# A graph network's first layer: one more block gathered, one fewer multiplied, and blocks built in another order

## The chip, the cores and the metric

The kernel runs on one core of one Trainium2 chip. The metric is the device time of one execution in microseconds (us); smaller is better. The engines are called by the profile's names: PE (matrix multiplies; PEld its weight loads), DVE (VectorE), ACT (ScalarE), POOL (GpSimd) and SP (which issues most DMAs).

## The reference

Four layers of message passing over 6250 nodes of 256 channels with 100000 edges sorted by destination, behind a layer norm and in front of a residual add:

```python
def agg(h):
    return jax.ops.segment_sum(h[src], dst, num_segments=N)      # N = 6250, 100000 edges
h = jnp.maximum(_layernorm(x), 0.0)
for l in range(3):
    t = h + agg(h)
    t = relu(t @ W1s[l] + b1s[l]); t = relu(t @ W2s[l] + b2s[l])
    h = t @ W3s[l] + b3s[l]
t = h + agg(h)
t = relu(t @ cW1 + cb1); t = relu(t @ cW2 + cb2)                 # cW2: 256 x 64
return x + t @ cW3 + cb3
```

## The kernel before

Nodes are cut into 49 blocks of 128. A layer's sum over edges is made in one of two ways for each block of destinations:

- A **gathered** block is made by a *visit*. POOL sends 17 indirect DMAs (L1407, `rows<-table,idx`), each of which fetches 128 source rows from the layer's table in DRAM; then PE adds them with 23 multiplications by a matrix of zeros and ones (L1446, `sums<-rows,hot`). `gath` has 24 buffers for such rows.
- A **multiplied** block uses its block row of the adjacency matrix: 49 matrices of 128 x 128 edge counts, each multiplied with one block of `XY` (the features as two halves, 512 columns). In the first layer these are 49 *products* of 128x512 at L1622 (`agg<-XY,a`); in later layers four blocks go together (L1700).

The adjacency counts are not given; they are **built** during the first layer for 30 blocks (18 to 47). For one block `build` runs 16 batches of two *steps*. For a batch DVE writes two tiles of zeros and ones, `lo` and `hi` (L1053, two buffers each). A step is two multiplications of 128x196 on PE (L1094, `bp<-hi,lo`, three buffers in PSUM) and one copy of the result into the block's counts `at` (three buffers): ACT copies the first step of a batch (L1102), DVE the second (L1104). DVE's order in a batch is `lo` and `hi` of the next batch, then the copy. A finished block is written to DRAM (SP, `mat<-at`) for the later layers; where the first layer multiplies it, ACT also turns it into 13 tiles `a` (L1582): twelve carry four products, the last one product. A tile with its products is called a *unit*.

Instructions stand in the order that the program text gives (no scheduler). A planner in Python decides that order: it counts units (`now`) and a clock worked out from fixed costs (`clock`), places visits and the two-stage dense layers (L1256, L1313) between units, and before each unit emits build steps:

```python
total = GSUB * len(made)
g0, u1 = GSUB + EARLY, steps - len(node_parts[-1]) - AHEAD - 1
goals = [min(g0 + (total - g0) * u // u1, total) for u in range(1, steps + 1)]
...
goal = min(goals[at - PRE], built[0] + 3)
while built[0] < goal and free_of(built[0] // GSUB - 3):
    next(beside)
    built[0] += 1
```

So the number of steps built follows a straight line over the units, at most three steps go ahead of one unit, and a block may be begun only when the block three places earlier in the list `made` has been turned into its `a` tiles (a block that the first layer doesn't multiply counts as free at once). `made` is the order in which blocks are built. `teams` are the multiplied blocks of the first layer, put through the dense layers together; `teams[0]` also decides how many blocks of the group 16 to 19 are gathered.

For visits, `begin` sets a pace at which rows are asked for and visits fall due; the plan ends `TAIL[l]` clock units ahead of the layer's worked-out end:

```python
self.end = begun[self.l] + work_of(self.l) - TAIL[self.l]
self.pace = (self.end - clock[0] - MARGIN) / self.upto[-1]
```

Of the kernel before, what the change touches and what calls it, by code (L numbers as in the profile page):

```python
# [396 lines left out]
def sorted_edges(  # L397
# [41 lines left out]
    NLAYER = W1s.shape[0]  # L439
# [29 lines left out]
    panels = [(20, 4), (24, 4), (28, 4), (32, 4), (36, 4), (40, 4), (44, 4)]  # L469
# [3 lines left out]
    S0 = 2 * min(place_of)  # L473


    teams = [(18, 2), (20, 4), (24, 4), (28, 4), (32, 4), (36, 4), (40, 2), (42, 2)]
    made = [b + i for b, n in teams for i in range(n)]
    for i in range(panels[-1][1]):
        made.insert(6 * i + 5, panels[-1][0] + i)
    assert sorted(made) == sorted(place_of) and sum(gone[-3]) == panels[0][0] and gone[-2] == panels[-1] and all(n == gone[0][1] for _, n in gone[:-1]) and sorted(  # L480
        b + i for b, n in gone[:-2] + gone[-1:] + panels for i in range(n)) == list(range(NT))
    NQ = len(gone)
# [498 lines left out]
    with tc.manual_schedule():  # L981
# [376 lines left out]
        class Gathered:  # L1358
# [30 lines left out]
            def begin(self):  # L1389
                self.one_hots(0)  # L1390
                self.end = begun[self.l] + work_of(self.l) - TAIL[self.l]
                self.pace = (self.end - clock[0] - MARGIN) / self.upto[-1]
# [139 lines left out]
        spare = clT.rearrange("p a q s -> p (a q s)").bitcast(F32)  # L1532
        sums = ps_g.tile([P, W], F32, name="sums")
        MARGIN = 6.0
        TAIL = [10.0] + [-5.0] * (NLAYER - 1) + [10.0]
        LATE = [-8] + [10] * (NLAYER - 1) + [-8]
        COLS, FULL32, TURN, VISIT, BUILD, BURST = 0.457e-3, 1.68e-3, 0.4, 3.0, 0.2, 0.3
        clock = [0.0]
# [10 lines left out]
        def work_of(l):  # L1549

            t = (len(nodes) if l == 0 else sum(stock[p][1] for p in order[l])) * NT * W * COLS
            t += len(layers[l].blocks) * (len(ROUNDS) * VISIT + TURN)
            for k, n in ((l, NT - tails[l]), (l - 1, tails[l - 1])):
                mid = NOUT if k == NLAYER else C
                t += (k >= 0) * n * (P * KC + C) * FULL32 * (2 if mid == C else 0.5)
            t += 2 * (len(gone) + (len(teams) if l == 0 else len(panels)) - 1) * BURST
            if l == 0:
                t += BUILD * GSUB * len(made) + TURN * len(nodes)
            return t
# [205 lines left out]
def kernel(  # L1765
# [26 lines left out]
    good = keep.tile([1, 1], I32, name="good")  # L1792
    rest = (x, src, dst, W1s, b1s, W2s, b2s, W3s, b3s, cW1, cb1, cW2, cb2, cW3, cb3, out)
    sorted_edges(tc, good, *rest)
    done = nc.values_load(good[0:1, 0:1], min_val=0, max_val=1)
    with tc.If(done == 0):
# [27 lines left out]
```

## Time and profile before

| | us |
|---|---|
| median of 3 runs | 2127.4 (2123.55 to 2129.25) |
| profiled execution, its own time | 2128.08 |
| profiled execution, its span | 2126.3 |
| PE busy in the span | 2034.3 |
| DVE busy | 925.0 |
| ACT busy | 872.8 |
| POOL busy | 1445.9 |

The span has three parts: normalisation and look-up of edges to about 116 us, the first layer to 690.8 us (the first L1700 product), and three later layers. Instructions of one kind are grouped by their source line; "idle before" is the time for which the engine stood still just ahead of them, and the name behind it is what ended that. A timeline row gives the start, the length, the line and the tiles, and in brackets the idle time ahead.

### The profile page before, as it was taken

Reading aid. Unit: us, or ns where it says so; the run is one execution under the profiler, and the core shown is the slowest. Engines: PE = TensorE matmul, PEld = TensorE weight load, DVE = VectorE, ACT = ScalarE, POOL = GpSimd, SP = SyncE. Lnnn points to the kernel's source line nnn. Section 1 sums busy time; section 2 is a strip of 40 time slices with the busy share of each in tenths; the row PEclk is TensorE's granted clock in tenths of the full one; section 3 lists DMA queues with packets and bytes.
Section 4 is the critical chain, followed back from the end, with each engine's and each line's share of the span. In section 5 each row is a group of like instructions: output and inputs, shape, how many; then the busy total and the mean of one; then the engine's idle time right before and its main releaser. Section 6 shows DMA issues by size and latency. Waiting matters only on the chain.

```text
span 2126.3 us, 33236 instructions
## 1 busy us (share of the span) xinstructions
PE 2034.3 (96%) x12076; PEld 1495.9 (70%) x12076; DVE 925.0 (44%) x2103; ACT 872.8 (41%) x1793; POOL 1445.9 (68%) x1467
## 2 busy tenths in 40 slices
PE   6889999999999999999999999999999999989998
PEld 4657676667676777777777777777776767766665
DVE  6987767677662422232234322322233323223333
ACT  5766656456555433323233423232233322222222
POOL 3747777677774477777777477777776477777772
PEclk9989999999999999999999999999999999999999
DMA  5534455545455654555566554555555555555563
GB/s 174 159 117 148 145 156 150 157 139 162 140 161 168 205 163 145 160 177 161 154 184 202 171 165 149 176 166 158 169 171 176 173 170 185 161 184 185 154 189 109
DMA packets 184900, 347.54 MB, mean 163 GB/s; under 512 B 32446, under 2 KB 118496, under 8 KB 184726
## 3 DMA queue, kind: packets, MB, share of 16 engines
q0 software_dynamic: 68960, 185.36, 29.9%
q1 hardware_dynamic: 113838, 158.12, 22.8%
q8 instruction: 96, 1.57, 0.3%
q10 hardware_dynamic: 1928, 1.85, 0.3%
q14 instruction: 78, 0.64, 0.1%
HBM read 287.93 MB, written 57.26 MB: 162 GB/s over the span
## 4 chain that ended last, share of the span: by engine, by line
PE 86%; DMA 4%; DVE 3%; issue 1%; ACT 1%; POOL 1%; DVEq 0%; SPq 0%; POOLq 0%; ACTq 0%
PE agg L1700 43%; PE agg L1622 15%; PE sums L1446 11%; PE ps L1256 6%; PE ps L1313 6%; PE bp L1094 4%; DMA rows<-table,idx 4%; PE ps L1506 1%; DVE hi L1053 1%; POOL rows L1407 1%; DVE at L1104 1%; PE ps L1268 1%; PE ps L1248 0%; DVE lo L1053 0%; ACT at L1102 0%
## 5 line engine op out<-in xcount | busy, mean ns | idle before, releaser
L1407 POOL DMA_INDIRECT rows<-table,idx x1394 | 1388.8, 996 | 595.7 <-issue 225.7
L1700 PE MATMUL agg<-a,XY 128*128 128x512 f32 x4116 | 978.6, 395 | 1.9 <-DVE clT L1634 1.9
L1700 PEld LDWEIGHTS agg<-a,XY 128*128 128x128 f32 x4116 | 764.9, 188 | 192.7 <-issue 35.0
L1598 ACT CAST a<-at 128x512 fp32r<-128x512 uint8 (+1 forms) x542 | 328.7, 617 | 653.7 <-PE agg L1700 613.1
L1598 DVE CAST a<-at 128x512 fp32r<-128x512 uint8 x543 | 246.8, 456 | 515.7 <-PE agg L1700 479.1
L1622 PE MATMUL agg<-XY,a 128*128 128x512 f32 x1470 | 405.4, 410 | 1.7 <-ACT a L1582 1.0
L1622 PEld LDWEIGHTS agg<-XY,a 128*128 128x128 f32 x1470 | 260.0, 190 | 51.4 <-issue 6.6
L1446 PE MATMUL sums<-rows,hot 128*32 128x256 f32 x3772 | 248.3, 391 | 33.5 <-DMA rows<-table,idx 33.3
L1446 PEld LDWEIGHTS sums<-rows,hot 128*32 128x32 f32 x3772 | 124.0, 111 | 151.0 <-DMA rows<-table,idx 46.1
L1582 ACT CAST a<-at 128x512 fp32r<-128x512 uint8 (+2 forms) x362 | 197.2, 576 | 6.6 <-PE agg L1622 6.6
L1102 ACT CAST at<-bp 128x392 uint8<-128x392 f32 x252 | 121.5, 490 | 186.9 <-PE bp L1094 181.3
L1104 DVE CAST at<-bp 128x392 uint8<-128x392 f32 x228 | 128.6, 564 | 137.4 <-PE bp L1094 135.0
L1475 DVE TENSOR_TENSOR u<-u,sums 128x256 f32<-128x256 f32 x82 | 34.4, 419 | 301.3 <-PE agg L1700 273.6
L1094 PE MATMUL bp<-hi,lo 128*128 128x196 bf16 x960 | 128.3, 256 | 14.9 <-DVE hi L1053 13.3
L1313 PE MATMUL ps<-w,h 128*128 128x256 f32 x588 | 133.8, 379 | 1.4 <-ACT h L1259 0.9
L1053 DVE TENSOR_TENSOR hi<-cols,pairs 128x784 bf16<-128x784 bf16 x240 | 134.9, 562 | 0.0
L1256 PE MATMUL ps<-h,w 128*128 128x512 f32 (+3 forms) x332 | 133.8, 545 | 0.3 <-ACT h L1713 0.3
L1094 PEld LDWEIGHTS <-lo 128*128 128x128 bf16 x960 | 72.3, 100 | 83.5 <-DVE hi L1053 34.9
L1313 PEld LDWEIGHTS ps<-w,h 128*128 128x128 f32 x588 | 111.3, 190 | 18.5 <-ACT h L1259 1.4
L1321 DVE TENSOR_TENSOR zz<-ps,w 128x512 f32<-128x512 f32 (+1 forms) x75 | 50.2, 679 | 116.5 <-PE ps L1313 116.5
L1053 DVE TENSOR_TENSOR lo<-lanes,pairs 128x512 bf16<-128x512 bf16 x240 | 100.6, 419 | 0.7 <-issue 0.3
L1510 ACT ACTIVATE h<-ps,bias 128x256 f32<-128x256 f32 (+1 forms) x116 | 47.6, 464 | 128.5 <-PE ps L1506 128.5
(170 smaller groups left out, 962.6 us busy)
## 6 DMA issues: line engine op xcount, KB each, us to landing
at<-mat SPq DMA_DIRECT2D x151, 448.0 KB
mat<-at SPq DMA_DIRECT2D x30, 784.0 KB
rows<-table,idx POOLq DMA_INDIRECT x1394
table<-zz SPq DMA_DIRECT2D x72, 256.0 KB
back<-table SPq DMA_DIRECT2D x99, 128.0 KB
xs<-in_x_dram SPq DMA_DIRECT2D x8, 768.0 KB
table<-zs SPq DMA_DIRECT2D x24, 256.0 KB
out_dram<-zz SPq DMA_DIRECT2D x24, 256.0 KB
```

The lines of the kernel that those rows point to most:

```text
L1053: nc.vector.tensor_tensor(o.rearrange("p q (n t) -> p q n t", t=2), values.rearrange("p (n t) -> p n t", t=2)[:, None, :, :].to_broadcast( ...
L1094: mm = nc.tensor.matmul(bp[:, m * HW:(m + 1) * HW], lo[:, q + m, :], hi[:, q + m, :], start=True, stop=True)
L1102: nc.scalar.copy(o, v)
L1104: nc.vector.tensor_copy(o, v)
L1256: mm = nc.tensor.matmul(ps[:mp, :w], weights[l][0][:, c, i * P:i * P + mp], h1[:, c, :w], start=(c == 0), stop=(c == KC - 1))
L1313: mm = nc.tensor.matmul(o, h2[0][:, c, nodes], w3[:, c, :], start=(c == 0), stop=(c == KC - 1))
L1407: got = nc.gpsimd.indirect_dma_start(out=t, out_offset=None, in_=tables[self.l][:, :], in_offset=bass.IndirectOffsetOnAxis(ap=idx[:, o:o + ...
L1446: nc.tensor.matmul(self.sums[m * Q:(m + 1) * Q, :C], self.hot[:, c - min(rounds), m, :], self.rows[g, c + 4 * m], start=(c == ROUNDS[0][0] ...
L1582: nc.scalar.copy(a[:, i * m * P:(i + 1) * m * P].rearrange("p (j d) -> p j d", j=m), counts[b][:, j:j + m, :])
L1598: cast(o, at[:, :, d:d + m * P])
L1622: mm = nc.tensor.matmul(agg, a[:, d:d + P], XY[:, j, :], start=(j == 0), stop=(j == NT - 1))
L1700: mm = nc.tensor.matmul(agg[c][:, :w], XY[:, j, o:o + P], a[:, :w], start=(at == 0 and half == 0), stop=(at == NT - 1 and half == 1))
```

## The change

Block 18 moves from the multiplied blocks to the gathered ones, so that 24 are gathered and 25 multiplied. Its counts are still built, since the last layer multiplies it, but last of all instead of first. The four blocks 44 to 47, built and not multiplied in the first layer, each stand one place later among the others. The plan of visits of the first layer ends 16 clock units ahead of the layer's worked-out end, not 10.

```diff
-    teams = [(18, 2), (20, 4), (24, 4), (28, 4), (32, 4), (36, 4), (40, 2), (42, 2)]
+    teams = [(19, 1), (20, 4), (24, 4), (28, 4), (32, 4), (36, 4), (40, 2), (42, 2)]
     made = [b + i for b, n in teams for i in range(n)]
     for i in range(panels[-1][1]):
-        made.insert(6 * i + 5, panels[-1][0] + i)
+        made.insert(6 * i + 6, panels[-1][0] + i)
+    made.append(18)
@@
-        TAIL = [10.0] + [-5.0] * (NLAYER - 1) + [10.0]
+        TAIL = [16.0] + [-5.0] * (NLAYER - 1) + [10.0]
```

From the `append` on, each line of the changed kernel has a number one higher (L1622 is L1623, L1094 is L1095).

Three places show how the rows move. The names are tiles with their numbers; `x4` is four instructions in a row.

PE in the middle of the first layer, before: one unit's four products, then two build steps (four multiplications and their weight loads), then the next four products.

```order
L1622 MATMUL agg_6094<-XY_71,a_6023 128x512 x4
L1094 LDWEIGHTS lo_6096
L1094 MATMUL bp_6124<-hi_6102,lo_6096 128x196
L1094 LDWEIGHTS lo_6096
L1094 MATMUL bp_6124<-hi_6102,lo_6096 128x196
L1094 LDWEIGHTS lo_6096
L1094 MATMUL bp_6130<-hi_6102,lo_6096 128x196
L1094 LDWEIGHTS lo_6096
L1094 MATMUL bp_6130<-hi_6102,lo_6096 128x196
L1622 MATMUL agg_6094<-XY_71,a_6031 128x512 x4
```

PE in the middle of the first layer of the changed kernel: these twelve rows are all that stands between four products ahead of them and one product behind them.

```order
L1095 LDWEIGHTS lo_5569
L1095 MATMUL bp_5591<-hi_5575,lo_5569 128x196
L1095 LDWEIGHTS lo_5569
L1095 MATMUL bp_5591<-hi_5575,lo_5569 128x196
L1095 LDWEIGHTS lo_5569
L1095 MATMUL bp_5597<-hi_5575,lo_5569 128x196
L1095 LDWEIGHTS lo_5569
L1095 MATMUL bp_5597<-hi_5575,lo_5569 128x196
L1095 LDWEIGHTS lo_5589
L1095 MATMUL bp_5605<-hi_5595,lo_5589 128x196
L1095 LDWEIGHTS lo_5589
L1095 MATMUL bp_5605<-hi_5595,lo_5589 128x196
```

Three build steps stand ahead of one unit where two stood. Behind the first 24 steps, 216 units have two steps ahead of them before and 8 have three; in the changed kernel 102 have three, 70 have two and 10 have one.

PE a few rows further on in the changed kernel: one build step, and then units with none.

```order
L1095 LDWEIGHTS lo_5649
L1095 MATMUL bp_5692<-hi_5655,lo_5649 128x196
L1095 LDWEIGHTS lo_5649
L1095 MATMUL bp_5692<-hi_5655,lo_5649 128x196
L1623 MATMUL agg_5613<-XY_71,a_5609 128x512 x4
L1623 MATMUL agg_5613<-XY_71,a_5637 128x512 x4
L1623 MATMUL agg_5613<-XY_71,a_5667 128x512 x4
L1623 MATMUL agg_5613<-XY_71,a_5698 128x512 x4
L1623 MATMUL agg_5613<-XY_71,a_5704 128x512 x4
L1623 MATMUL agg_5613<-XY_71,a_5714 128x512 x4
L1623 MATMUL agg_5613<-XY_71,a_5722 128x512 x4
```

After a stretch of groups of three steps, seven units follow each other without a step; before, the units without a step stood one by one between the others.

SP's DMAs at the end of the first layer, before (`mat_95` holds the counts of blocks 40 to 43, `mat_90` those of 20 to 23, `table_84` is the second layer's table, and `back` brings rows of it back to be split):

```order
L516 DMA table_84<-zz 128x2x256 x2
L1109 DMA mat_95<-at 896x1x896 x2
L516 DMA table_84<-zz 128x2x256
L1109 DMA mat_95<-at 896x1x896
L1127 DMA at<-mat_90 128x3584
L516 DMA back<-table_84 128x256 x5
L516 DMA table_84<-zz 128x2x256 x2
L516 DMA back<-table_84 128x256 x7
```

SP's DMAs at the same place of the changed kernel:

```order
L517 DMA table_84<-zz 128x2x256 x2
L1110 DMA mat_95<-at 896x1x896 x3
L517 DMA table_84<-zz 128x2x256
L517 DMA table_84<-zz 128x256
L1128 DMA at<-mat_90 128x3584
L517 DMA back<-table_84 128x256 x3
L1110 DMA mat_97<-at 128x6272
L517 DMA table_84<-zz 128x2x256 x2
L517 DMA back<-table_84 128x256 x9
```

The write of block 18's counts (`mat_97`) was the first of all such writes and is now the last, with two table writes and nine `back` reads behind it. POOL asks for 408 tiles of rows in the first layer where it asked for 391, and PE has 49 products of L1622 fewer and 23 multiplications of L1446 more. From the first L1700 product on, PE's rows are the same in both kernels.

## The prediction, made blind

> **What bounds the kernel now.** I read the page first, then the busy time by stage, the waits and groups of the first layer, and the timelines of PE and DVE where a few microseconds decide.
>
> ```profile
> span 2126.3 us, 33236 instructions
> PE 2034.3 (96%) x12076; PEld 1495.9 (70%) x12076; DVE 925.0 (44%) x2103; ACT 872.8 (41%) x1793; POOL 1445.9 (68%) x1467
> ```
>
> PE bounds the whole. By windows (start and end, length, then busy time of PE, PEld, DVE, ACT and POOL with the number of instructions, granted clock, DMA share, GB/s):
>
> ```profile
> 116.00:122.00 6.00, 0.77 (x9) 0.69 (x10) 4.79 (x14) 0.80 (x3) 1.15 (x1) 0.75 0.13 37
> 122.00:134.00 12.00, 9.86 (x50) 5.24 (x48) 10.84 (x27) 10.42 (x27) 7.60 (x7) 0.50 0.60 200
> 200.00:640.00 440.00, 432.24 (x2940) 304.42 (x2940) 308.45 (x697) 258.71 (x584) 323.22 (x323) 1.00 0.51 152
> 549.20:554.20 5.00, 4.33 (x31) 3.02 (x30) 4.41 (x12) 3.68 (x9) 3.78 (x5) 1.00 0.75 228
> ```
>
> In the body of the first layer PE is busy 432.2 of 440 us and DVE 308.5: DVE has 30% to spare as a mean. The second layer's order on PE is unchanged, so the whole difference is made here. The only PE waits in the first layer that matter are two (total, times, longest):
>
> ```profile
> PE bp L1094 <- DVE hi L1053: 7.2, 12, 1.4
> PE sums L1446 <- DMA rows<-table,idx: 2.4, 1, 2.4
> ```
>
> The first, 7.2 us between 134 and 640 us, is PE waiting for DVE's ones-and-zeros tiles. The last row of the windows is one such place, where before already has two groups of three build steps one after the other. PE there:
>
> ```profile
> 549.25 0.69 PE L1094 MATMUL bp<-hi,lo 128*128 128x196 bf16 x6
> 549.71 1.18 PE L1622 MATMUL agg<-XY,a 128*128 128x512 f32 x4
> 550.73 0.34 PE L1094 MATMUL bp<-hi,lo 128*128 128x196 bf16 x2
> 551.23 0.51 PE L1094 MATMUL bp<-hi,lo 128*128 128x196 bf16 x4 [0.16 <-DVE hi L1053]
> 551.53 1.17 PE L1622 MATMUL agg<-XY,a 128*128 128x512 f32 x4
> 552.54 0.51 PE L1094 MATMUL bp<-hi,lo 128*128 128x196 bf16 x4
> 552.84 0.48 PE L1622 MATMUL agg<-XY,a 128*128 128x512 f32 x1
> 553.83 0.51 PE L1094 MATMUL bp<-hi,lo 128*128 128x196 bf16 x4 [0.51 <-DVE hi L1053]
> ```
>
> And DVE, which is idle at first and then never:
>
> ```profile
> 549.80 0.57 DVE L1104 CAST at<-bp 128x392 uint8<-128x392 f32 x1 [0.59 <-PE bp L1094]
> 550.28 0.41 DVE L1053 TENSOR_TENSOR lo<-lanes,pairs 128x512 bf16<-128x512 bf16 x1
> 550.61 0.56 DVE L1053 TENSOR_TENSOR hi<-cols,pairs 128x784 bf16<-128x784 bf16 x1
> 551.11 0.57 DVE L1104 CAST at<-bp 128x392 uint8<-128x392 f32 x1
> 551.93 0.56 DVE L1053 TENSOR_TENSOR hi<-cols,pairs 128x784 bf16<-128x784 bf16 x1
> 552.40 0.56 DVE L1104 CAST at<-bp 128x392 uint8<-128x392 f32 x1
> 553.21 0.56 DVE L1053 TENSOR_TENSOR hi<-cols,pairs 128x784 bf16<-128x784 bf16 x1
> 553.69 0.56 DVE L1104 CAST at<-bp 128x392 uint8<-128x392 f32 x1
> ```
>
> Copy to copy is 1.29 us (551.11, 552.40, 553.69): that is DVE's price of a batch (two build steps). PE starts a batch's first row 0.05 to 0.06 us after DVE ends its `hi` (551.17, 552.49 and 553.77, against 551.23, 552.54 and 553.83). On PE six building multiplications, three steps, take 0.46 us (549.25 to 549.71), so a step is 0.15; four products take 1.02 (549.71 to 550.73), one takes about 0.32. A unit with two steps therefore costs PE 0.30 + 1.02 = 1.32 us and DVE 1.29: balanced, and the units without steps between them let DVE catch up. A unit with three steps costs PE 1.47 and DVE 1.94.
>
> **The change part by part.**
>
> *Products and visit.*
>
> ```profile
> 651.49 2.80 PE L1446 MATMUL sums<-rows,hot 128*32 128x256 f32 x46
> 654.22 5.74 PE L1622 MATMUL agg<-XY,a 128*128 128x512 f32 x24
> 659.80 0.60 PE L1506 MATMUL ps<-ident,un 128*128 128x128 f32 x4
> ```
>
> 24 products take 659.80 - 654.22 = 5.58 us, 0.2325 each; 49 fewer give -11.4 us. One more visit costs 654.22 - 651.49 = +2.7 us. Block 18's transposes and dense layers move from a pair to a group of three and leave block 19 alone; the columns are the same: 0. ACT loses 13 casts and isn't waited for: 0.
>
> *The end of the plan.* The last visit of the layer waited 2.4 us for its rows. The changed plan paces rows so that they end 6 units sooner; I take the wait as gone, -2.4, between -2.4 and 0.
>
> *The build steps.* This is the term that decides. The steps are the same 480, but in the changed order they stand in 102 groups of three (8 before), because the straight line of the plan is now steeper (as many steps over 13 units fewer) and 18 and 44 to 47 stand further back: the builder gets to its limit of three `at` buffers, stops, and makes up for it at three steps a unit when a block's casts are through. A run of such groups is bound by DVE. How much PE waits follows from the place above. When a run starts, the tiles of the first two batches are ready. DVE begins the first copy 0.55 us after PE's first build row (549.25 to 549.80), so batch i (from 0) can start at 0.55 + (i - 1) x 1.29 + 0.06, the last for the step from DVE to PE; for i = 2, 3 and 4 that is 1.90, 3.19 and 4.48 us, and the trace has 1.98, 3.29 and 4.58 (551.23, 552.54, 553.83). PE alone would be there after 0.15 per step and the products between. With "n" the groups that follow each other without a visit or a dense layer between:
>
> - n = 2 (last batch is i = 2): ready 1.90, PE alone 1.62; wait 0.3. There are 5: 1.5 us.
> - n = 3 (i = 4): ready 4.48, PE alone 3.24, or 2.54 where one unit has a single product; wait 1.2 (four) or 1.9 (one): 6.7 us.
> - n = 4 (i = 5): ready 5.77, PE alone 3.86 with a single-product unit; wait 1.9 (three), 1.2 (one): 6.9 us.
> - n = 5 (i = 7; the usual one, most of a block in one go): ready 8.35; PE alone 14 x 0.15 + 3 x 1.02 + 0.32 = 5.5; wait 2.9. There are 9: 26.1 us.
> - n = 9, once: ready 0.61 + 12 x 1.29 = 16.1, PE alone 11.4; 4.7 us. Seven groups stand alone: 0.
>
> That is 45.9 us of new waiting, in runs that last 9.5 + 22.4 + 23.1 + 75.2 + 16.1 = 146 us together. PE doesn't get it back: in the stretches without steps it runs at its own rate, and there DVE idles, since its two buffers of `lo` and `hi` let it be one batch ahead and no more.
>
> *DVE's other work in those runs.* In the body of the layer (134 to 640 us):
>
> ```profile
> L1430 DVE TENSOR_TENSOR hot<-colf,rel 128x768 f32<-128x768 f32 x21 | 20.0, 952 | 0.0
> L1321 DVE TENSOR_TENSOR zz<-ps,w 128x512 f32<-128x512 f32 x18 | 11.6, 682 | 0.0
> L1634 DVE TENSOR_TENSOR un<-un,agg 128x256 f32<-128x256 f32 x23 | 9.6, 415 | 1.3 <-ACT un L1630 1.3
> L1466 DVE TENSOR_TENSOR u<-XY 128x256 f32<-128x256 f32 x21 | 8.8, 419 | 3.7 <-PE ps L1506 3.7
> L1475 DVE TENSOR_TENSOR u<-u,sums 128x256 f32<-128x256 f32 x21 | 8.7, 413 | 0.0
> L1108 DVE TENSOR_TENSOR at<-at,ident 128x128 uint8<-128x128 uint8 x28 | 8.2, 293 | 4.2 <-ACT at L1102 1.2 <-ACT pairs L1048 0.5
> ```
>
> 66.9 us in 506, or 0.13 us in each. What falls into a run adds to the wait in full: 146 x 0.13 = 19; a little less, since these rows overlap the next one's start: I take +16, between 0 and 30 (they may cluster between runs or in them).
>
> *Waits of before.* The 7.2 us belong to units of two and three steps; of those with two, 70 are left of 216. I take -4.8, between -7.2 and 0.
>
> *POOL and SP.* POOL has 17 tiles more to ask for:
>
> ```profile
> L1407 POOL DMA_INDIRECT rows<-table,idx x362 | 363.7, 1005 | 145.6 <-issue 57.8 <-PE bp L1094 43.7 <-PE agg L1622 34.0
> 663.25 0.96 POOL L1407 DMA_INDIRECT rows<-table,idx  x1 [0.30 <-issue]
> 664.52 0.95 POOL L1407 DMA_INDIRECT rows<-table,idx  x1 [0.31 <-issue]
> ```
>
> At its fastest it asks every 1.27 us (663.25 to 664.52); 408 x 1.27 = 518 us. The layer gave it 506 us for 362, or 1.40 each, and will be longer: 0.
>
> ```profile
> mat<-at SPq DMA_DIRECT2D x30, 784.0 KB
> ```
>
> On SP the write of block 18's counts (784 KB, at the 228 GB/s of the fourth window about 3.5 us of transfer) now stands ahead of the last table writes; its block is complete over 20 us sooner by PE's order (at least 52 products of 0.23 and a visit stand between), so I give it 0, and up to 3.
>
> The sum: -11.4 + 2.7 - 2.4 + 45.9 + 16 - 4.8 = +46.0 us. The profiled execution took 2128.1 (span 2126.3), 0.7 above the median of the runs, so 2128.1 + 46.0 = 2174.
>
> **The rivals.**
>
> *DVE stays hidden.* If the steps' tiles were ready anyway, only PE's own work would count: 2128.1 - 11.4 + 2.7 - 2.4 = 2117. For it: DVE is idle 30% of the body as a mean, and the two waits at the place above are small. Against it: that place shows DVE without a pause from 549.80 and PE held by it at the third and the fifth batch; the mean says nothing of a run. It would decide if runs were of one or two groups, but 19 of the 31 are longer. Chance 0.04.
>
> *Half of it.* If runs are cut up by waits elsewhere (a late `a` tile, a full PSUM buffer), so that DVE catches up inside them: half of 45.9 + 16, 2128.1 - 11.4 + 2.7 - 2.4 - 4.8 + 31 = 2143. Chance 0.08.
>
> *PE's clock falls.* In a run of five PE works 5.5 of 8.35 us, 66%. The windows show 1.00 granted at 87% (4.33 of 5.00 us) and 0.50 right after a stretch at 13% (0.77 of 6.00): 66% lies between, nearer to the first, and with gaps of under 1 us each. At half clock the five units of a run would take PE 11 us where DVE takes 8.35: 2.7 more a run, and for 102 groups, twenty times five, +54: 2228. Chance 0.04. The Trainium skill has this rule in "TensorE: Matmul & The Clock Gate", under "A second HAM failure mode: psum-queue depth-cycling": small idle gaps between groups of multiplications can make the clock swing between half and full. By that rule the time would be 2228; the fourth window, with such gaps at full clock, speaks against it here.
>
> **How the numbers follow.** The forecast has 0.83: 2174. Its own bounds: small DVE work 0 and all of the old waits gone, -11.4 + 2.7 - 2.4 - 7.2 + 45.9 = +27.6, or 2156; small work 30, none of the old waits or of the last visit's gone and SP's 3, -11.4 + 2.7 + 45.9 + 30 + 3 = +70, or 2198. The other cases lie outside (2117 and 2143 below, 2228 above) and have 0.16 together, 0.01 is left for what I don't see, so the range of 2156 to 2198 has about 8 in 10. A change of 0.3% (6 us) is about what a measurement of this kernel can tell from none. Faster by more than that: 0.04, the hidden DVE. Within: 0.01. Slower: 0.95.
>
> **What the profile after would show.** PE's wait for DVE's `hi` at L1095 should grow from 7.2 to some 60 to 70 us, in clusters of 3 to 4 us, once for nearly each multiplied block, with DVE's copies 1.29 us apart in them. PE's busy time should fall by about 9 us, the first L1701 product should come near 737 us instead of 690.8 (below), and what lies behind it should last as long as before. I am wrong if PE's wait for `hi` stays under 30 us, if the granted clock in the body of the first layer falls below 0.95, or if visits wait for rows.
>
> ```profile
> 690.81 1.21 PE L1700 MATMUL agg<-a,XY 128*128 128x512 f32 x4 [1.85 <-DVE clT L1634]
> ```

## The result, and the profile after

| | before | after |
|---|---|---|
| median of 4 runs, us | 2125.48 (2123.44 to 2129.25) | 2182.88 (2174.47 to 2184.61) |
| profiled execution, own time, us | 2128.08 | 2174.47 |
| span, us | 2126.3 | 2172.7 |
| first layer, 116 us to the first product of the second, us | 574.8 | 626.9 |
| from there to the end of the span, us | 1435.5 | 1429.8 |

The ratio is 1.0257 with a 95% interval of 1.0232 to 1.0282: slower, by some 49 to 60 us between medians. The profiled execution of the changed kernel was the shortest of its four; profile against profile the loss is 46.4 us. Only the profiled one can be looked into, so the accounting below is of 46.4; where the others spend 7 to 10 us more is not known. The mean granted clock doesn't tell: it is 0.986 in the profiled execution and 0.985 in the others, which is about 2 us by estimate.

The page's busy times of the changed kernel:

```profile
PE 2041.0 (94%) x12073; PEld 1495.5 (69%) x12073; DVE 923.8 (43%) x2105; ACT 877.1 (40%) x1782; POOL 1464.3 (67%) x1484
```

The waits of PE over its whole span (total, times, longest):

```profile
PE bp L1095 <- DVE hi L1054: 60.5, 87, 5.2
PE sums L1447 <- DMA rows<-table,idx: 24.8, 14, 4.5
```

The same two waits over the whole span of before:

```profile
PE sums L1446 <- DMA rows<-table,idx: 33.3, 15, 6.2
PE bp L1094 <- DVE hi L1053: 13.3, 15, 5.2
```

The wait for DVE's `hi` has grown by 47.2 us (60.5 against 13.3), all of it in the first layer; DVE as a whole has no more to do than before. The first product of the second layer in the changed kernel:

```profile
742.86 1.16 PE L1701 MATMUL agg<-a,XY 128*128 128x512 f32 x4 [2.00 <-ACT a L1599]
```

It comes 52.0 us later than the 690.81 of before. The rest is 5.6 us shorter, which is about what visits waited less for their rows there (24.8 in the changed kernel, all of it in the later layers; 33.3 before, of which 2.4 in the first).

The two stages as windows. The first row is the first layer of the changed kernel, the second that of before (columns as in the prediction):

```profile
116.00:742.90 626.90, 559.98 (x3673) 389.27 (x3671) 388.06 (x886) 342.65 (x780) 413.24 (x408) 0.97 0.47 141
```

```profile
116.00:690.80 574.80, 553.41 (x3667) 389.77 (x3667) 387.43 (x883) 341.97 (x791) 393.20 (x391) 0.98 0.50 150
```

PE is idle for 66.9 us where it was for 21.4, and its busy time rose by 6.6, though 49 products are gone.

**One run, row by row.** PE in one of the nine runs of five groups of three (behind the third group stands one product, behind the others four; the two rows left out are that product and the first two rows of the fourth group):

```profile
580.28 0.68 PE L1095 MATMUL bp<-hi,lo 128*128 128x196 bf16 x6
580.75 1.18 PE L1623 MATMUL agg<-XY,a 128*128 128x512 f32 x4
581.77 0.34 PE L1095 MATMUL bp<-hi,lo 128*128 128x196 bf16 x2
582.65 0.52 PE L1095 MATMUL bp<-hi,lo 128*128 128x196 bf16 x4 [0.54 <-DVE hi L1054]
582.95 1.18 PE L1623 MATMUL agg<-XY,a 128*128 128x512 f32 x4
583.97 0.52 PE L1095 MATMUL bp<-hi,lo 128*128 128x196 bf16 x4
586.09 0.34 PE L1095 MATMUL bp<-hi,lo 128*128 128x196 bf16 x2 [1.61 <-DVE hi L1054]
...
587.38 0.83 PE L1095 MATMUL bp<-hi,lo 128*128 128x196 bf16 x4 [0.50 <-DVE hi L1054]
587.91 2.06 PE L1623 MATMUL agg<-XY,a 128*128 128x512 f32 x4
589.77 1.20 PE L1095 MATMUL bp<-hi,lo 128*128 128x196 bf16 x6
```

DVE in the same run, its copies and what comes between them:

```profile
580.89 0.57 DVE L1105 CAST at<-bp 128x392 uint8<-128x392 f32 x1 [8.59 <-issue]
...
581.71 0.41 DVE L1476 TENSOR_TENSOR u<-u,sums 128x256 f32<-128x256 f32 x1
582.04 0.56 DVE L1054 TENSOR_TENSOR hi<-cols,pairs 128x784 bf16<-128x784 bf16 x1
582.51 0.56 DVE L1105 CAST at<-bp 128x392 uint8<-128x392 f32 x1
...
583.80 0.56 DVE L1105 CAST at<-bp 128x392 uint8<-128x392 f32 x1
584.27 0.95 DVE L1431 TENSOR_TENSOR hot<-colf,rel 128x768 f32<-128x768 f32 x1
585.14 0.42 DVE L1054 TENSOR_TENSOR lo<-lanes,pairs 128x512 bf16<-128x512 bf16 x1
...
585.95 0.56 DVE L1105 CAST at<-bp 128x392 uint8<-128x392 f32 x1
...
587.24 0.56 DVE L1105 CAST at<-bp 128x392 uint8<-128x392 f32 x1
...
588.52 0.57 DVE L1105 CAST at<-bp 128x392 uint8<-128x392 f32 x1
588.99 0.42 DVE L1635 TENSOR_TENSOR un<-un,agg 128x256 f32<-128x256 f32 x1
589.32 0.43 DVE L1054 TENSOR_TENSOR lo<-lanes,pairs 128x512 bf16<-128x512 bf16 x1
589.66 0.57 DVE L1054 TENSOR_TENSOR hi<-cols,pairs 128x784 bf16<-128x784 bf16 x1
```

DVE had stood idle for 8.59 us, and now works without a gap. Copies are 1.29 us apart (582.51 to 583.80, 585.95 to 587.24), 1.62 where the sum into `u` falls between them and 2.15 where a `hot` does. So `u` adds 0.33 (581.71 to 582.04), `hot` 0.87 (584.27 to 585.14), and `un` at the end 0.33. PE's 1.61 us of wait at 586.09 is that `hot` on top of 0.74. By the prediction's working batch 5 is ready 5.77 us after the run's first row, with `u` and `hot` 6.97; PE begins it at 587.38, 7.10 behind 580.28. The last batch's `hi` should end after 8.35 - 0.06 + 0.33 + 0.87 + 0.33 = 9.82 us; it ends at 590.23, after 9.95.

**What the idle column leaves out.** The two building rows that begin at 581.77 are shown for 0.34 us, to 582.11, and the wait behind them as 0.54. In a row without a wait two such rows take 0.15. So 0.19 of the hold is counted as busy; at 583.97, with four rows shown for 0.52 where the next thing starts after 0.30, it is 0.22. With 72 waits more (87 against 15) at 0.2, some 14 us of the hold stand in PE's busy time. This is an estimate: the 0.2 was read at these two places only.

**The clock.** Three windows of 10 us of the changed kernel:

```profile
430.00:440.00 10.00, 9.51 (x46) 7.38 (x45) 6.49 (x16) 6.38 (x14) 6.08 (x6) 0.83 0.43 127
510.00:520.00 10.00, 7.45 (x37) 4.89 (x37) 9.37 (x23) 5.41 (x12) 6.03 (x6) 0.83 0.32 101
580.00:590.00 10.00, 7.35 (x41) 4.73 (x41) 9.11 (x21) 5.31 (x12) 6.79 (x8) 0.87 0.32 93
```

Before, the same three windows had 1.00. The row of 587.91 shows it directly: four products end after 1.86 us (587.91 to 589.77) instead of 1.02. The layer has five such slow groups of four from 140 us on; that is 5 x 0.84 = 4.2 us. Build rows are slower there too (four of them take 0.53 from 587.38, where four take 0.30 at full clock). The trace grants 0.50 in four stretches, from 430.4, 512.3 and 587.4 for 3.4 us each and from 696.6 for 6.8 us; these are 17 us, of which half, 8.5 us, is the most that the clock can have cost. Before has one stretch of 3.4 us in the same part of the layer. In the run above it cost nothing: PE needed the last batch's `hi` two steps later, and that was there only at 590.23. Without the slow products PE would have waited for it.

The 3.4 us just ahead of each of the four falls, and a fifth stretch that brought none:

```profile
427.00:430.40 3.40, 1.51 (x11) 0.69 (x9) 3.40 (x8) 1.60 (x5) 2.02 (x3) 1.00 0.33 94
508.90:512.30 3.40, 0.93 (x7) 0.48 (x7) 3.40 (x8) 1.85 (x5) 2.79 (x3) 1.00 0.59 181
584.00:587.40 3.40, 1.29 (x11) 0.68 (x11) 3.40 (x8) 1.60 (x6) 2.61 (x3) 1.00 0.35 94
693.20:696.60 3.40, 1.73 (x12) 0.87 (x10) 3.40 (x10) 2.60 (x8) 2.58 (x3) 1.00 0.35 94
477.30:480.70 3.40, 0.94 (x7) 0.50 (x7) 3.40 (x8) 1.83 (x5) 2.45 (x3) 1.00 0.45 131
```

Ahead of each fall PE was busy for 0.93 to 1.73 us of 3.40, that is 27 to 51%. In the fifth stretch it was busy for 28% with pauses of 0.77 and 1.69 us, and kept its clock, so neither the pauses nor the share decide alone. The times of the four falls differ by 81.9, 75.1 and 109.2 us, which is 24, 22 and 32 times 3.41 us. That fits a clock that is set anew every 3.41 us by what PE did in the interval before; these few falls suggest it and don't prove it.

### The profile page after: what moved, and what is told of

Read it like the earlier page. It is cut to its first block, busy times and chain, and to the rows that moved or that the text cites. A ratio compares the mean times of both kernels' runs of the same rounds, so it can differ in the third digit from the quotient of the medians.

```text
span 2172.7 us, 33325 instructions
## 1 busy us (share of the span) xinstructions
PE 2041.0 (94%) x12073; PEld 1495.5 (69%) x12073; DVE 923.8 (43%) x2105; ACT 877.1 (40%) x1782; POOL 1464.3 (67%) x1484
## 4 chain that ended last, share of the span: by engine, by line
PE 80%; DVE 9%; DMA 3%; issue 2%; ACT 1%; POOL 1%; DVEq 0%; ACTq 0%; SPq 0%; POOLq 0%
PE agg L1701 42%; PE agg L1623 12%; PE sums L1447 10%; PE ps L1314 6%; PE ps L1257 6%; DVE hi L1054 3%; DMA rows<-table,idx 3%; DVE at L1105 2%; PE bp L1095 2%; DVE lo L1054 2%; PE ps L1507 1%; POOL rows L1408 1%; DVE hot L1431 1%; PE ps L1249 0%; PE ps L1269 0%
## 5 line engine op out<-in xcount | busy, mean ns | idle before, releaser
L1408 POOL DMA_INDIRECT rows<-table,idx x1411 | 1407.3, 997 | 622.2 <-issue 227.6
L1599 ACT CAST a<-at 128x512 fp32r<-128x512 uint8 x543 | 330.8, 619 | 660.6 <-PE agg L1701 631.2
L1599 DVE CAST a<-at 128x512 fp32r<-128x512 uint8 (+1 forms) x542 | 244.1, 452 | 528.9 <-PE agg L1701 494.0
L1623 PE MATMUL agg<-XY,a 128*128 128x512 f32 x1421 | 390.4, 412 | 2.3 <-DVE un L1635 1.3
L1623 PEld LDWEIGHTS agg<-XY,a 128*128 128x128 f32 x1421 | 257.5, 192 | 54.9 <-issue 8.2
L1447 PE MATMUL sums<-rows,hot 128*32 128x256 f32 x3818 | 249.5, 389 | 24.8 <-DMA rows<-table,idx 24.8
L1583 ACT CAST a<-at 128x512 fp32r<-128x512 uint8 (+2 forms) x349 | 189.5, 572 | 47.2 <-PE agg L1623 46.5
L1095 PE MATMUL bp<-hi,lo 128*128 128x196 bf16 x960 | 133.7, 261 | 62.1 <-DVE hi L1054 60.5
L1095 PEld LDWEIGHTS <-lo 128*128 128x128 bf16 x960 | 72.5, 101 | 135.8 <-DVE hi L1054 96.5
L1257 PE MATMUL ps<-h,w 128*128 128x512 f32 (+4 forms) x332 | 133.8, 545 | 0.3 <-ACT h L1714 0.3
```

Of the source, the lines that this page charges most:

```text
L1095: mm = nc.tensor.matmul(bp[:, m * HW:(m + 1) * HW], lo[:, q + m, :], hi[:, q + m, :], start=True, stop=True)
L1257: mm = nc.tensor.matmul(ps[:mp, :w], weights[l][0][:, c, i * P:i * P + mp], h1[:, c, :w], start=(c == 0), stop=(c == KC - 1))
L1408: got = nc.gpsimd.indirect_dma_start(out=t, out_offset=None, in_=tables[self.l][:, :], in_offset=bass.IndirectOffsetOnAxis(ap=idx[:, o:o + ...
L1447: nc.tensor.matmul(self.sums[m * Q:(m + 1) * Q, :C], self.hot[:, c - min(rounds), m, :], self.rows[g, c + 4 * m], start=(c == ROUNDS[0][0] ...
L1583: nc.scalar.copy(a[:, i * m * P:(i + 1) * m * P].rearrange("p (j d) -> p j d", j=m), counts[b][:, j:j + m, :])
L1599: cast(o, at[:, :, d:d + m * P])
```

## The experiments

The runs below were made in three sets, one each on the chips numbered 6, 8 and 0; the number of the chip of the result above, called the first chip here, is not known. In all three sets the kernel before takes 2395 to 2397 us and not 2125, so ratios to the kernel before of the same set are compared. The ratios in the table are not quotients of the medians, which differ from them by up to 0.2%. The changed kernel there (e1) shows waits that the profile puts down to "issue", time in which the engine waited for nothing that the profile shows:

```profile
PE sums L1447 <- issue: 79.7, 141, 1.7
PE bp L1095 <- DVE hi L1054: 53.2, 59, 5.2
PE bp L1095 <- issue: 15.6, 23, 3.0
```

My theory: groups of three build steps make PE wait for DVE's tiles. The rivals: the later end of the plan (`TAIL`), the later place of 44 to 47, and PE's clock. Two parts of the change have no run of their own: block 18 built last, and the 24th visit in the place of its products.

| run | kernel | ratio to before, 95% | first layer, us | wait for `hi` in it, us |
|---|---|---|---|---|
| first set: e1_after_again | changed | 1.0206 (1.0163 to 1.0250) | 703 | 53.2 |
| e2_two_steps | changed, two steps a unit | 1.0094 (1.0061 to 1.0128) | 677 | 22.7 |
| e3_copies_act | changed, half of DVE's copies to ACT | 1.0163 (1.0117 to 1.0208) | 685 | 43.0 |
| e4_before_later_44 | before, 44 to 47 later | 1.0009 (0.9987 to 1.0031) | 652 | 18.5 |
| second set: e5_two_steps_act | e2 and e3 together | 1.0114 (1.0096 to 1.0133) | 678 | 14.6 |
| e6_two_steps_b | e2 again | 1.0119 (1.0098 to 1.0139) | 679 | 24.8 |
| e7_filled_gaps | changed, more work on PE in the gaps | 1.0259 (1.0235 to 1.0284) | 708 | 40.3 |
| e8_tail10 | changed, `TAIL` 10 | 1.0250 (1.0223 to 1.0278) | 702 | 43.1 |
| third set: e9_two_no_single | changed, two steps, none at single products | 1.0127 (1.0091 to 1.0162) | 677 | 17.8 |
| e10_two_no_single_act | e9 and e3 together | 1.0116 (1.0082 to 1.0150) | 670 | 9.9 |
| e11_before_no_three | before, no group of three | 1.0005 (0.9982 to 1.0028) | 655 | 13.6 |
| e12_before_bunched | before, steps bunched | 1.0005 (0.9982 to 1.0029) | 640 | 14.6 |

The first layer is that of one profiled execution, from 116 us to the first product of the second layer.

**The changed kernel again** (no edit), for comparison.

> The changed kernel as it is, beside the others of this set. The profiled execution took 2174.5 us and three more 2182 to 2185. If DVE's tiles alone hold PE (theory), every execution should wait some 55 us for them and the time should lie within 2174 to 2185. If PE's clock has a share that changes from run to run (rival), the granted clock is lower in the slower executions.

2447.65 us against 2394.59. Its first layer is 51.5 us longer than that of e4, which differs from before by nothing measurable; on the first chip the change cost 52.1 there. The loss between the medians is 53.1 us, much like on the first chip. The slowest execution (2457.2) has the lowest granted clock (0.965), but the other three (0.968 to 0.972) don't follow that order, and only the slowest was profiled; the question of what varies is not settled.

**Two steps a unit.**

```diff
-                    goal = min(goals[at - PRE], built[0] + 3)
+                    goal = min(goals[at - PRE], built[0] + 2)
```

> The changed kernel with at most two build steps ahead of a unit. Theory (runs of three steps are bound by DVE): a unit of two steps costs PE 1.32 us and DVE 1.29, so only the unit with a single product (0.62 against 1.29, once a block) and DVE's small work still cost: about 1 us a block over 24 blocks, less the 9 us of PE work saved: 2135, between 2125 and 2145. Rival (the order of the blocks or the 24th visit itself costs the time): it stays at 2174 to 2185.

With no group of three left, 25 us are back in the set (2422.29 against 2447.65), and 35 in the second set (2424.20 of e6 against 2459.37 of e8, which has groups of three). Waits in the first layer of e2:

```profile
PE bp L1095 <- issue: 26.6, 32, 3.2
PE bp L1095 <- DVE hi L1054: 22.7, 27, 5.3
PE bp L1095 <- ACT at L1103: 12.7, 14, 1.7
```

The wait for `hi` fell from 53.2 to 22.7, near the 18.5 of e4. So the groups of three are about half of the loss on these chips, and the wait for DVE with them. The other half stays; the forecast, at most 0.9% behind before, was just missed in this set (0.94%).

**A cheaper batch for DVE.** ACT takes three of four copies, not one of two.

```diff
-                    if step % 2 or step <= 2 * PRE:
+                    if step % 4 or step <= 2 * PRE:
```

> The changed kernel with its runs of three steps, but DVE makes one of four copies of built counts and ACT three (before, each made every second one). Theory: DVE's price of a batch falls from 1.29 to about 1.05 us, a run of five groups ends at 0.61 + 6 x 1.05 = 6.9 instead of 8.35 us and waits 1.4 instead of 2.9: half of the waits goes, 2174 - 25 = about 2150, between 2145 and 2165. Rival (PE waits for something else in those runs, such as its clock or PSUM): no change, or slower, as ACT copies come later.

2434.44 against 2447.65, and the executions of the two don't overlap (2432 to 2440 and 2446 to 2457). DVE's first-layer busy time fell by 50 us (339.7 against 389.9), the wait for `hi` by 10. The gain of 13 us is half of the 25 that were forecast. DVE's price of a batch is thus shown to matter in runs of three; it is not shown to be all of it.

**44 to 47 alone.** The kernel before, with only the change of places.

```diff
-        made.insert(6 * i + 5, panels[-1][0] + i)
+        made.insert(6 * i + 6, panels[-1][0] + i)
```

> The kernel before with one part of the change alone: blocks 44 to 47 each built one place later. The order then has 24 groups of three steps where before has 8, and nothing else changes. Theory: 16 groups more at about 0.45 us each (45.9 us for 102 groups), +5 to +8 us: 2131 to 2133. Rival (where the blocks stand doesn't matter): 2125.

2397.29 against 2394.59: nothing that can be told from zero. It has 24 groups of three instead of 8; that they would cost 5 to 8 us did not show, though the interval (up to 1.0031, or 7 us) doesn't exclude most of that.

**Both edits** of e2 and e3 (e5), and the edit of e2 alone once more in the same set (e6).

> The changed kernel with at most two build steps ahead of a unit, and with DVE making one of four copies of built counts where it made every second. Theory: DVE's price of a batch is then about 1.05 us against PE's 1.32 for a unit with two steps, so PE's waits for DVE nearly go and the 8.7 us of saved PE work remain: 0.2 to 0.4% faster than the kernel before (2118 to 2123 where that takes 2125). Rival (ACT, with three copies of four and the casts, takes DVE's place): no better than the two-step kernel without this, 0.4 to 1% slower than before.

> [...] Theory: 2125 to 2145 where before takes 2125, that is at most 1% slower, with PE's wait for DVE at 20 to 30 us. Rival (not the groups of three): 2.3% or more slower.

Both forecasts missed: e5 is 1.1% slower than before and not faster, and e6 1.2% where at most 1% was said. With 14.6 us of wait for `hi` against the 24.8 of e6, e5 takes 2423.34 us where e6 takes 2424.20. What is left once the groups of three are gone is not DVE's price of a batch.

**Work for PE in the gaps**, to hold its clock: three more multiplications of 128x256, whose results nobody uses, ahead of the third step of a unit.

```diff
                    goal = min(goals[at - PRE], built[0] + 3)
+                    since = built[0]
                     while built[0] < goal and free_of(built[0] // GSUB - 3):
+                        if built[0] - since == 2:
+                            for _ in range(3):
+                                nc.tensor.matmul(sums[:, C:], XY[:, 1, :P], XY[:, 0, :C], start=True, stop=True)
```

> The changed kernel with three extra multiplications of 128x256 (0.11 us each) ahead of the third build step of each group of three; their results go to an unused half of a PSUM bank. They fill part of the 0.5 us in which PE waits in each such group. If only DVE's price counts (theory), nothing is gained and what isn't hidden is lost: up to 10 us slower than the changed kernel, 2180 to 2195, and PE's wait for DVE falls by some 25 us. If PE's halved clock after such gaps has a share (rival), the granted clock stays at 1.00 in the first layer and the time falls by 5 to 10 us, to 2165 to 2177.

The body of the first layer of e7, and of e8, which has no such work and ran on the same chip (it has `TAIL` 10, too; the changed kernel as it is was not run in this set):

```profile
200.00:640.00 440.00, 386.66 (x2552) 273.42 (x2551) 244.65 (x551) 208.07 (x457) 267.26 (x271) 0.98 0.41 124
```

```profile
200.00:640.00 440.00, 372.14 (x2343) 254.63 (x2345) 245.78 (x556) 208.71 (x458) 275.42 (x270) 0.95 0.41 124
```

The clock rose from 0.95 to 0.98 and PE's busy time by 14.5 us, and the time was the same, 2461.0 against 2459.4. The wait for `hi` fell by 3 us (40.3 against 43.1) and not by the 25 that were forecast, though PE's idle time in the layer as a whole fell by 22 (89.7 against 111.4). So a low clock is not shown to carry the loss. A part can't be excluded: over the layer the clock is 0.96 against 0.94, which is up to 14 us of 700 by estimate, and the fillers' own work may have taken as much.

**The end of the plan.**

```diff
-        TAIL = [16.0] + [-5.0] * (NLAYER - 1) + [10.0]
+        TAIL = [10.0] + [-5.0] * (NLAYER - 1) + [10.0]
```

> The changed kernel with the plan of visits ending 10 units ahead of the layer's end, as before. Theory: the groups of three stay (102) and so does the time, within 5 us of the changed kernel. Rival (visits or row requests pushed together are the cost): 20 us or more faster than the changed kernel.

1.0250 against the 1.0206 of the changed kernel in the other set, with intervals that overlap; the 20 us or more that the rival gives are not there: no sign that `TAIL` has a part in the loss. What `TAIL` does is seen in a single wait: with 10, PE waits once in the first layer for a visit's rows (2.8 us in e8), with 16 in e1 it doesn't.

**What is left of the loss.** Four kernels. The first two take from the changed kernel also the steps ahead of a unit of one product, and the last two rearrange the steps of the kernel before.

```diff
-                    goal = min(goals[at - PRE], built[0] + 3)
+                    goal = min(goals[at - PRE], built[0] + (2 if m > 1 else 0))
-        TAIL = [16.0] + [-5.0] * (NLAYER - 1) + [10.0]
+        TAIL = [13.0] + [-5.0] * (NLAYER - 1) + [10.0]
```

> The changed kernel with at most two build steps ahead of a unit of four products, none ahead of the unit of one product, and TAIL 13 instead of 16. Theory (DVE's price of a batch decides, also in what is left of the loss with two steps a unit): a unit of one product with two steps costs PE 0.30 + 0.32 us and DVE 1.29, so about 0.67 us of wait for each of some 21 such units, 14 us; without them 2424 - 14 = 2410 where before takes 2397, ratio 1.005 (1.003 to 1.007), and PE's wait for hi falls by 8 us or more. Rival (what is left is the price of PE's own instruction supply, which groups of steps draw on wherever they stand): 1.010 to 1.012, as with two steps a unit.

> As the run before it, and DVE takes one of four of the copies to at instead of one of two (ACT the others). Theory (DVE's price): DVE's price of a batch falls by about a quarter, the rest of its wait goes: 6 to 10 us less than the run before it, ratio 1.001 to 1.003. Rival (instruction supply): no difference from the run before it, within 0.2%.

The wait for `hi` fell by 5 to 7 us to 17.8 (e9), a little less than the 8 forecast, and to 9.9 (e10). The time did not fall: 2427.66 and 2425.60, no better than two steps a unit. The theory is refuted for this half of the loss. The times are those that the rival gave; that its cause, PE's instruction supply, is the right one is not shown (below).

For e11 the first of these two edits stands alone in the kernel before; for e12 it reads

```diff
-                    goal = min(goals[at - PRE], built[0] + 3)
+                    goal = min(goals[at - PRE], built[0] + (2 if l or j0 < 40 else 0))
```

> The kernel before, with no group of three steps and no step ahead of a unit of one product: 228 groups of two. Theory: its eight groups of three and the single-product units cost it a few microseconds of wait for hi: 1 to 4 us less, ratio 0.998 to 1.000. Rival: those waits are covered by others: 1.000 to 1.003.

> The kernel before, with two steps at most ahead of a unit and none ahead of the last three units of each block: the same 228 groups of two as in the run before it, in runs of up to ten units with three empty units behind. Theory (a unit with two steps is balanced, 1.32 us of PE against 1.29 of DVE, so that only the small work of DVE in the runs counts): 0 to 5 us more than the run before it, ratio 1.000 to 1.002 to the kernel before. Rival (runs of groups of two cost as such, on the instruction supply): 10 to 20 us more, 1.004 to 1.008.

Both equal the kernel before, within 0.3%. So neither its eight groups of three nor bunching of the kind in e12 is worth anything measurable, and such bunching isn't what keeps e2, e6 and e9 1% behind. First-layer waits of e9, and behind them those of e12:

```profile
PE bp L1095 <- issue: 30.6, 29, 3.7
PE bp L1095 <- DVE hi L1054: 17.8, 21, 5.2
PE sums L1447 <- issue: 12.0, 19, 1.1
```

```profile
PE bp L1094 <- issue: 16.8, 23, 2.8
PE bp L1094 <- ACT at L1102: 16.6, 16, 2.6
PE bp L1094 <- DVE hi L1053: 14.6, 18, 5.2
```

The waits put down to "issue" are the part that is larger in e9, 42.6 us with the visits' against 17.6. But e11, as fast as e12 over its runs, has 31.8, and its profiled execution is 15 us longer in this layer. So one profile of each kernel can't tell what is to be explained from what varies. Against e11 the layer of e9 is 22 us longer and PE idle for 20 us more (92.5 against 72.3), spread over several waits, the largest part being "issue" ahead of visits' multiplications (12.0 against 2.6). Nor do the traces show that "issue" is a want of instructions: the DMA queue that the profile's page calls `instruction` has the same 96 packets and 0.3% in e1 as in the changed kernel on the first chip. What holds back a changed kernel with two steps a unit on these chips **stays open**. On the first chip PE's waits in this layer contain no "issue", and no kernel with two steps a unit was run there, so whether it would match the kernel before on that chip isn't known either. None of the twelve beat the kernel before.

## Why the prediction was right

It said 2174, with 2156 to 2198; the median is 2182.88 and the profiled execution 2174.47. The range held and the mechanism is seen in the trace; that the middle fits the profiled execution so closely is luck, since two misses of about 6 us, in the first layer and behind it, cancel. Step by step, on the first chip:

- **The build steps**, +45.9 and +16, less 4.8 of old waits: 57.1. Measured: 47.2 us of idle time, and some 14 (the estimate above) in the ends of instructions just ahead of waits, 61 together. The mechanism is the one forecast: copies 1.29 us apart, DVE idle before a run and never in it, PE held at the third, fifth and sixth batch. In the run above small work fell into the wait in full, as its `hot` and `u` show; other runs were not taken apart like this. That the groups of three are the cause was tested in the three later sets only; there they carry the wait for DVE and half of the loss.
- **The clusters** were to be 3 to 4 us each. In the run above PE's waits are 0.54 + 1.61 + 0.50 = 2.65, and 0.6 more in the ends. In the layer from 134 to 690 us:

```profile
PE bp L1095 <- DVE hi L1054: 52.7, 80, 2.0
```

  These are 80 waits of 0.66 us, several to a cluster. 52.7 is less than the 60 to 70 that this row was to reach from 7.2; with the 0.2 us of each end it comes to some 69, by estimate.
- **Products and visit**, -8.7. They can't be read from PE's busy time, which rose by 6.6: 6.6 + 8.7 = 15.3 us, which the ends (14) and the slow products (4) fill within 3 us, both by estimate. The forecast that busy time would fall by about 9 was wrong. It took the hold for idle time alone.
- **The last visit's wait for rows**, -2.4: gone from the first layer, as forecast. In the later sets it is back with `TAIL` 10 (2.8 us in e8).
- **The later part**, forecast the same, took 5.6 us less, since its visits waited 6.1 us less for rows (24.8 against 30.9). I had no step for that; the first layer lost 52.1 and not the forecast 46.
- **PE's clock**, a rival at 0.04: it falls in places and not for the whole layer. The body has 0.99 as a mean, with 0.83 to 0.87 in the windows shown, and the cost is some 4 us in products and 8.5 at most, not 54. The rival's 66% was the mean of a run; just ahead of the falls PE was busy for 27 to 51% of 3.40 us. The Trainium skill says in "TensorE: Matmul & The Clock Gate", "A second HAM failure mode: psum-queue depth-cycling", that short idle times between groups of multiplications, if they come often enough, make the clock swing between half and full. The trace agrees: here the clock fell behind pauses of 0.5 to 1.6 us.
- **DVE hidden** and **half of it** fell with the wait of 60.5.

The median lies 8.4 us above the profiled execution, so the agreement of 2174 with 2174.47 is partly chance, too: the ratio's interval begins at 1.0232, and the forecast was 1.0216.

## What to carry to other kernels

Price a helper engine by the stretch in which it is called on, not by its mean: a unit that asks 1.94 us of DVE while PE has 1.47 of its own work makes PE wait even where DVE is idle for 38% of the layer (388.06 us busy of 626.90). Work that is taken off PE isn't gained if the steps that remain have to fit into fewer units; here 11.4 us of products went and the layer became 52 us longer. In a trace like this one, add about 0.2 us to each of such short waits of PE for the end of the instruction ahead, which the busy column counts.

## What the hardware showed that was not expected

- PE's granted clock fell in a layer where PE is busy for 89% of the time (559.98 of 626.90 us): behind pauses of 0.5 to 1.6 us four products took 1.86 us instead of 1.02. Ahead of each of the four falls PE was busy for at most 51% of 3.40 us, and the falls lie whole multiples of 3.41 us apart; a stretch with 28% that lay elsewhere brought none.
- One kernel takes 2125 us on the first chip and 2395 to 2397 us in the three later sets. In e1 PE waits for "issue", 79.7 us ahead of visits' multiplications and 15.6 ahead of build steps, and its busy time is 156 us longer than on the first chip (2196.9 against 2041.0); why is not known. A timeline row there:

```profile
927.83 0.63 PE L1447 MATMUL sums<-rows,hot 128*32 128x256 f32 x4 [0.81 <-issue]
```

  It stands in the second layer, inside a visit; on the first chip the 46 multiplications of the row at 651.49 in the prediction follow each other without a pause.
